# Inverse square roots by Newton steps on VectorE in a four-layer kernel

## The chip, the core and the metric

The kernel runs on one core of a Trainium2 chip. The metric is the device time of one execution in microseconds (us). A core has a matrix engine (TensorE, PE in the profile, with its weight loads shown as PEld), VectorE (DVE), ScalarE (ACT), GpSimd (POOL) and SyncE (SP); each works through its own queue of instructions in order, and semaphores join them.

## What is computed

Four layers are applied to x, 4 x 256 tokens of 256 features, with a context of 4 x 1601 tokens. Each layer adds an attention and then a feed-forward network (FFN) to x, each on a layer-normalized x:

```python
def _layernorm(x, axis=-1, eps=1e-05):
    ...
    return (x - m) / jnp.sqrt(v + eps)
...
        def rms_norm(x, w, eps=EPS):
            var = jnp.mean(jnp.square(x), axis=-1, keepdims=True)
            return x * jax.lax.rsqrt(var + eps) * w
...
    x = x + _L0_xattn_ref(_layernorm(x, axis=-1), ctx_2048, mask_BxS2_bk0)
    x = x + _L0_ffn_ref(_layernorm(x, axis=-1), ...
    x = x + _L1_xattn_ref(_layernorm(x, axis=-1), ctx_2048, ...
    x = x + _L1_ffn_ref(_layernorm(x, axis=-1), ...
    x = x + _L2_xattn_ref(_layernorm(x, axis=-1), ctx_2048, ...
    x = x + _L2_ffn_ref(_layernorm(x, axis=-1), ...
    x = x + _L3_xattn_ref(_layernorm(x, axis=-1), ctx_2048, ...
    x = x + _L3_ffn_ref(_layernorm(x, axis=-1), ...
```

Inverse square roots come in two kinds. A layer normalization needs one for each token. Layers 2 and 3 also normalize each head's query and key by its root mean square: in layer 2 there are 16 query heads and 4 key heads of 128 features, with the keys made from context and tokens; in layer 3 there are 32 heads of 8 features, with keys and values from the context alone. The FFNs are a mixture of 32 experts (layer 0), of 8 with a shared one (layer 1), of 4 (layer 2), and one with quantized weights and activations (layer 3).

## The kernel before, in words

Tokens lie on the 128 partitions; a batch b of 256 tokens is two tiles (q = 0, 1). The four layers run one after the other, and a good deal is pulled forward: layer 2's context keys and values (16 units of batch and key head) are computed as filler for PE (`fill`, tiles fill and filly, `l2_early`, L1206) from layer 0 on and parked in memory. A tile scheduler orders each engine's queue by its own model of costs; only what goes through `pin` or `keep_in_program_order` keeps the written order. A change to a few instructions therefore moves others too.

In the profiled execution the stages lie as follows. Layer 0's attention takes 0 to 130 us and its FFN 130 to about 380. Adding the experts' results (`l0_add`, L544, the gather-adds of L558) and layer 1's attention (`l1_xattn`, L1195: a layer normalization, a summary vector added, a second normalization, then the result added to x at L1204) take about 380 to 516, and layer 1's FFN runs from there to about 625. Layer 2's attention is prepared until 700; its units run from 700 to 1724, about 64 us each. Layer 2's FFN takes 1724 to 1913, layer 3's attention 1913 to 2540, and the rest of its FFN, for the last batch, ends at 2569.

Before the change an inverse square root is `rstd` (L79): a Sqrt on ACT (L81) and a reciprocal on DVE (L82). ACT can evaluate a function only with its table loaded; the profile shows each load as ACT_TABLE_LOAD on the line that called for it. `layernorm` (L84) does bn_stats (L91) and bn_aggr (L92) for both tiles, one rstd, and a normalizing tensor_scalar for each (L95). Other calls are these:

- Layer 0's head (L317): statistics of batch 0, its rstd and transposed tokens; then the statistics of batches 1 to 3 and one rstd for their six tiles. The scores of a batch and tile are masked and their maximum taken by one DVE instruction (L261), the exp on ACT is L271. The decay factor `dec` takes an exp, and its scan on DVE and a DMA from ACT's queue build a row of weights.
- `l2_early`'s `norm` (L1262): one rstd of 13 columns for each early unit.
- Layer 2's `prep` (L1372) prepares a unit while the one before it runs: an rstd over 11 columns (3 key tiles and 8 query columns), then `exps_next` (L1350), a dummy exp that brings the exp table back, then `rq` (L1440), the queries' scaling on POOL (L1442), the keys' scaling on ACT (L1446), transposes (L1452) and copies of kT (L1459). Beside it, for each head, DVE takes the maxima (L1483), ACT the exp p (L1487), POOL scales p (L1522), DVE transposes p (pT, L1528) and PE multiplies by the values.
- Layer 3's `l3_kv` (L1668) makes the keys and values of a batch in 13 steps: two matmuls into a bank, then copies to kr (L1683) and va (L1685); after steps 4, 9 and 12 `l3_squares` (L1716) adds up the squares of 5, 5 and 3 steps (32 heads each, so 160, 160 and 96 columns). For batch 0 one rstd covers all key columns. For later batches the root waits for `queries` (L1779), which takes one Sqrt (L1810) over keys, queries and two columns for the normalization of an older batch, and reciprocals (L1811, L1816). POOL then scales kr.
- In the steady part of layer 3, PE computes the scores of a pair of key tiles, ACT their exp (L1943), PE the product with the values. A generator, `beside` (L1972), puts one piece of other work next to each pair: key and value steps of the next batch, its queries, the FFN of the batch before. These pieces share a single PSUM bank.

Of the kernel before, what the change touches and what calls it, by code (L numbers as in the profile page):

```python
# [11 lines left out]
F32 = mybir.dt.float32  # L12
# [4 lines left out]
I32 = mybir.dt.int32  # L17
AF = mybir.ActivationFunctionType
ALU = mybir.AluOpType
# [4 lines left out]
P = 128  # L24
# [5 lines left out]
NM = 13  # L30
# [10 lines left out]
NH2, NKV2, HD2 = 16, 4, 128  # L41
# [10 lines left out]
FIRST3 = [7, 1, 3]  # L52
# [6 lines left out]
class Kernel:  # L59
# [19 lines left out]
    def rstd(self, out, in_, scale, eps):  # L79

        self.nc.scalar.activation(out, in_, AF.Sqrt, bias=eps, scale=scale)  # L81
        self.nc.vector.reciprocal(out, out)  # L82

    def layernorm(self, out, x):  # L84

        nc = self.nc
        st = self.small.tile([P, 2, 6], F32, name="ln_st")
        mv = self.small.tile([P, 2, 2], F32, name="ln_mv")
        rs = self.small.tile([P, 2], F32, name="ln_rs")
        for q in range(2):  # L90
            nc.vector.bn_stats(st[:, q, :], x[:, q, :])  # L91
            nc.vector.bn_aggr(mv[:, q, :], st[:, q, :])  # L92
        self.rstd(rs, mv[:, :, 1], 1.0, self.eps5)
        for q in range(2):
            nc.vector.tensor_scalar(  # L95
                out[:, q, :], x[:, q, :], mv[:, q, 0:1], rs[:, q : q + 1],
                ALU.subtract, ALU.mult,
            )
# [67 lines left out]
    def l0_xattn(self):  # L166
        nc, tc, i = self.nc, self.tc, self.i
        with ExitStack() as es:
# [142 lines left out]
            for b0, b1 in ((0, 1), (1, B)):  # L311
                for b in range(b0, b1):
                    for q in range(2):
                        st = self.small.tile([P, 6], F32, name="st0")
                        self.pin(nc.vector.bn_stats(st, self.x[b][:, q, :]))
                        self.pin(nc.vector.bn_aggr(mv[:, b, q, :], st))
                self.rstd(rs[:, b0:b1], mv[:, b0:b1, :, 1], 1.0, self.eps5)  # L317
                if b0 == 0:
                    xT = turned(0)
            self.pin(nc.scalar.activation(dec, dec, AF.Exp, scale=-1.0))  # L320
# [885 lines left out]
    def l2_early(self, ctxT):  # L1206
# [88 lines left out]
    def l2_xattn(self):  # L1295
# [11 lines left out]
        with ExitStack() as es:  # L1307
# [42 lines left out]
            def exps_next():  # L1350

                self.pin(nc.scalar.activation(self.small.tile([P, 1], F32, name="one2"), self.eps6, AF.Exp))
# [19 lines left out]
            def prep(u, w, res):  # L1372
# [295 lines left out]
    def l3_kv(self, b, st, early):  # L1668


        nc = self.nc
        ctxT = self.ctx3
        pool = self.late3 if b % 2 else self.a3
        kr = st["kr"] = self.a3.tile([P, NM, D], F32, name="kr3")
        va = st["va"] = self.va3[b % 2]
        ss = st["ss"] = self.a3.tile([P, (NM + 2) * NH3 + 2], F32, name="ss3")
        for m in range(NM):
            copy = nc.scalar.copy if early() else nc.vector.tensor_copy
            tf = self.take()
            for k in range(2):  # L1680
                self.mm(tf, ctxT[:, k, m * P : (m + 1) * P], self.wkv3[:, k, :], k == 0, k == 1)
            tp = tf.rearrange("p (h d c) -> p h d c", d=HD3, c=2)
            copy(kr[:, m, :].rearrange("p (h d) -> p h d", d=HD3), tp[:, :, :, 0])  # L1683
            for h in range(2):
                copy(  # L1685
                    va[h][:, m, : 16 * (HD3 + 1)].rearrange("p (h e) -> p h e", e=HD3 + 1)[:, :, :HD3],
                    tp[:, h * 16 : (h + 1) * 16, :, 1],
                )
# [6 lines left out]
        if b == 0:  # L1695
            nk = NM * NH3
            self.rstd(ss[:, :nk], ss[:, :nk], 1.0 / HD3, self.eps6)
        for m0, m1 in ((0, 4), (4, 8), (8, 12), (12, NM)):
            v = kr[:, m0:m1, :].rearrange("p m (h d) -> p (m h) d", d=HD3)
            f = ss[:, m0 * NH3 : m1 * NH3, None].to_broadcast([P, (m1 - m0) * NH3, HD3])  # L1700
            nc.gpsimd.tensor_tensor(v, v, f, ALU.mult)
        yield
        yield
        yield
        kT = st["kT"] = [pool.tile([P, MP], F32, name="kT3", bufs=2) for _ in range(2)]
        for m0 in range(0, NM, 4):
            for h in range(2):
                n = min(4, NM - m0)
                copy = nc.scalar.copy if early() else nc.vector.tensor_copy
                tp = self.take().rearrange("p (m k) -> p m k", k=P)  # L1710
                for m in range(n):
                    nc.tensor.transpose(tp[:, m, :], kr[:, m0 + m, h * P : (h + 1) * P], self.ident)
                copy(kT[h][:, m0 * P : (m0 + n) * P], tp[:, :n, :].rearrange("p m k -> p (m k)"))
                yield

    def l3_squares(self, st, v, m0, early, pool=None):  # L1716

        n = v.shape[1]
        sq = (pool or self.a3).tile([P, 2 if pool else 5, D], F32, name="sqq3" if pool else "sq3")
        if early:  # L1720
            self.nc.scalar.activation(sq[:, :n, :], v, AF.Square)
        else:
            self.nc.gpsimd.tensor_tensor(sq[:, :n, :], v, v, ALU.mult)
        self.nc.vector.tensor_reduce(
            st["ss"][:, m0 * NH3 : (m0 + n) * NH3], sq[:, :n, :].rearrange("p m (h d) -> p (m h) d", d=HD3),
            AX.X, ALU.add,
        )

    def l3(self, first):

# [10 lines left out]
        with ExitStack() as es:  # L1741
# [16 lines left out]
            def stats(b):  # L1758
                for q in range(2):
                    t = self.small.tile([P, 6], F32, name="st3")  # L1760
                    nc.vector.bn_stats(t, self.x[b][:, q, :])
                    nc.vector.bn_aggr(mv[:, b, q, :], t)
# [9 lines left out]
            def norms(bs):  # L1772

                for b in bs:
                    stats(b)
                v = slice(bs[0], bs[-1] + 1)
                self.rstd(rs[:, v, :], mv[:, v, :, 1], 1.0, self.eps5)

            def queries(b, st, old=None, fill=lambda n: None):  # L1779

                ss = st["ss"]
                nk, nq = NM * NH3, (NM + 2) * NH3
                if old is not None:
                    stats(old)
                    nc.vector.tensor_scalar(
                        ss[:, nq:], mv[:, old, :, 1], float(HD3), HD3 * (1e-5 - 1e-6), ALU.mult, ALU.add
                    )
                elif b:  # L1790
                    nc.vector.memset(ss[:, nq:], 1.0)
                xn = normed(b, rs[:, b, :])
                fill(0)
                tp = bank().rearrange("p (k q t) -> p k q t", k=2, q=2)
# [19 lines left out]
                if b:  # L1814
                    for c in range(0, nk, nk // 2):
                        nc.vector.reciprocal(ss[:, c : c + nk // 2], ss[:, c : c + nk // 2])  # L1816
                fill(2)
                yield
                yield
# [152 lines left out]
            def beside(b, st):  # L1972

                if b + 1 < B:
# [40 lines left out]
            for _ in queries(0, first, None, lambda n: [next(kv) for _ in range(FIRST3[n])]):  # L2015
                pass
            busy = True
            self.take = bank
# [208 lines left out]
```

## Time and profile before

| | us |
|---|---|
| median of 3 runs | 2565.55 (2564.33 to 2566.97) |
| profiled execution | 2571.23 |
| its span | 2569.2 |
| granted TensorE clock in it, mean | 0.973 of full speed |

The profile shows one execution. The busy time of an engine is a sum over all stages, and it is work beside other work for the most part. What a stage is worth is read from what PE waits for in it: a row of the waits names the waiting tile and line, then what it waited for with its line, then the total in us, the number of times and the longest. A group row gives line, engine, operation, tiles and count, then busy us and mean ns of one, then the idle time of the engine just before it and what ended it. A timeline row gives start, duration, engine, line, operation and tiles, with idle time and releaser in brackets.

Busy PE in each stage, and its idle time:

| us | stage | PE busy | PE idle |
|---|---|---|---|
| 0 to 30 | head | 23.88 | 6.12 |
| 30 to 130 | layer 0's attention | 95.38 | 4.62 |
| 130 to 380 | layer 0's FFN | 229.69 | 20.31 |
| 380 to 480 | adding experts, layer 1's attention | 73.28 | 26.72 |
| 480 to 625 | its end, layer 1's FFN | 139.42 | 5.58 |
| 625 to 700 | preparing layer 2 | 66.96 | 8.04 |
| 700 to 1724 | layer 2's units | 1003.27 | 20.73 |
| 1724 to 1920 | layer 2's FFN | 187.03 | 8.97 |
| 1920 to 2130 | layer 3's start and batch 0 | 200.98 | 9.02 |
| 2130 to 2540 | layer 3, batches 1 to 3 | 398.30 | 11.70 |
| 2540 to 2569.2 | end of the last FFN | 11.44 | 17.76 |

### The profile page before, as it was taken

Reading aid. Unit: us, or ns where it says so; the run is one execution under the profiler, and the core shown is the slowest. Engines: PE = TensorE matmul, PEld = TensorE weight load, DVE = VectorE, ACT = ScalarE, POOL = GpSimd, SP = SyncE. Lnnn points to the kernel's source line nnn. Section 1 sums busy time; section 2 is a strip of 40 time slices with the busy share of each in tenths; the row PEclk is TensorE's granted clock in tenths of the full one; section 3 lists DMA queues with packets and bytes.
Section 4 is the critical chain, followed back from the end, with each engine's and each line's share of the span. In section 5 each row is a group of like instructions: output and inputs, shape, how many; then the busy total and the mean of one; then the engine's idle time right before and its main releaser. Section 6 shows DMA issues by size and latency. Waiting matters only on the chain.

```text
span 2569.2 us, 47086 instructions
## 1 busy us (share of the span) xinstructions
PE 2429.6 (95%) x17607; PEld 1507.7 (59%) x17623; DVE 1404.4 (55%) x2915; ACT 1310.9 (51%) x3000; POOL 837.8 (33%) x1516
## 2 busy tenths in 40 slices
PE   8989987899989999999999999998999999999997
PEld 5777865777645555555555555565554544544553
DVE  5453534843567777777777777763324324334323
ACT  3234434533654545454545454423336766757875
POOL 1015644213345555555555555541011001011000
PEclk9999998989999999999999999998999999999998
DMA  7165574624601111111111111004310100000000
GB/s 252 49 211 163 169 151 146 216 91 138 225 18 48 48 48 48 47 47 48 47 48 48 47 48 48 9 1 176 125 56 28 35 1 28 6 1 2 6 6 5
DMA packets 96474, 188.45 MB, mean 73 GB/s; under 512 B 15401, under 2 KB 64297, under 8 KB 95050
## 3 DMA queue, kind: packets, MB, share of 16 engines
q1 hardware_dynamic: 80102, 146.50, 16.7%
q0 software_dynamic: 10416, 28.46, 4.6%
q10 hardware_dynamic: 5732, 10.49, 1.3%
q8 instruction: 143, 2.34, 0.4%
q14 instruction: 81, 0.66, 0.1%
HBM read 137.29 MB, written 48.11 MB: 72 GB/s over the span
## 4 chain that ended last, share of the span: by engine, by line
PE 84%; DVE 5%; ACT 3%; DMA 3%; issue 2%; POOL 1%; another core or an unknown queue 1%; SPq 0%; ACTq 0%; PEld 0%; POOLq 0%; DVEq 0%; PEldq 0%
PE s L77 25%; PE o L77 24%; PE fill L1241 3%; PE f2gu L77 3%; PE b L77 3%; PE f1gu L77 2%; PE acc L77 2%; PE tpq L77 2%; PE f0gu L77 2%; PE filly L1241 2%; PE tpkv L77 2%; PE av L77 2%; PE f0y L77 2%; PE f2y L77 1%; PE f1y L77 1%
## 5 line engine op out<-in xcount | busy, mean ns | idle before, releaser
L1487 ACT ACTIVATE p<-s,nmsm 128x448 f32<-128x448 f32 (+1 forms) x512 | 326.1, 643 | 381.4 <-PE s L77 247.5
L1943 ACT ACTIVATE e<-s 128x1024 f32<-128x1024 f32 (+1 forms) x448 | 404.2, 960 | 159.6 <-PE s L77 154.5
L77 PE MATMUL o<-pT,va 128*128 128x256 f32 (+2 forms) x1920 | 434.2, 379 | 9.4 <-DVE pT L1528 7.9
L77 PE MATMUL s<-kT,qT 128*32 128x448 f32 (+1 forms) x4096 | 427.3, 558 | 11.6 <-ACT kT L1459 8.2
L77 PEld LDWEIGHTS o<-pT,va 128*128 128x128 f32 (+1 forms) x1920 | 347.5, 192 | 130.4 <-issue 89.6
L1522 POOL TENSOR_SCALAR p<-p,rm 128x448 f32<-128x448 f32 (+1 forms) x512 | 323.1, 651 | 6.2
L1483 DVE TENSOR_REDUCE nmsm<-s 128x2 f32<-128x896 f32 (+1 forms) x256 | 287.5, 1123 | 7.9
L77 PE MATMUL s<-qb,kT 32*128 32x256 f32 (+1 forms) x3328 | 268.2, 405 | 13.2 <-ACT e L1943 11.0
L1528 DVE STREAM_TRANSPOSE pT<-p 128x896 f32<-128x896 f32 (+1 forms) x256 | 270.7, 1111 | 9.4 <-POOL p L1522 8.7
L77 PEld LDWEIGHTS s<-kT,qT 128*32 128x32 f32 x4096 | 120.2, 110 | 264.0 <-issue 239.0
L77 PE MATMUL o<-e,va 128*32 128x256 f32 (+1 forms) x3328 | 236.3, 392 | 1.2 <-DVE os L2040 1.2
L77 PEld LDWEIGHTS s<-qb,kT 32*128 32x128 f32 (+1 forms) x3328 | 163.4, 181 | 105.2 <-issue 75.5
L1515 POOL TENSOR_TENSOR rm<-em,tot 32x8 f32<-32x8 f32 x256 | 54.2, 212 | 400.8 <-DVE tot L1512 389.6
L1241 PE MATMUL fill<-wkc_early,ctxT 128*128 128x256 f32 (+1 forms) x572 | 146.2, 407 | 13.4 <-ACT kT_early L1277 12.6
L77 PEld LDWEIGHTS o<-e,va 128*32 128x32 f32 (+1 forms) x3328 | 90.6, 110 | 115.1 <-issue 75.0
L1970 POOL TENSOR_TENSOR x<-x,t 128x32 f32<-128x32 f32 x64 | 14.7, 251 | 439.7 <-DVE t L1965 439.7
L1480 DVE TENSOR_TENSOR s<-s,mask 128x128 f32<-128x128 f32 (+1 forms) x256 | 84.3, 330 | 104.7 <-PE s L77 92.5
L1241 PEld LDWEIGHTS fill<-wkc_early,ctxT 128*128 128x128 f32 (+1 forms) x572 | 114.4, 203 | 35.4 <-ACT kT_early L1277 14.8
L458 POOL DMA_INDIRECT f0xr<-f0xd,f0src x95 | 90.5, 953 | 70.6 <-PE f0tph L515 18.7
L1487 ACT ACTIVATION_READ_ACCUMULATOR p<-s,nmsm 128x1 f32 x512 | 101.4, 198 | 0.0
L77 PE MATMUL f2gu<-f2wgu,f2xsT 128*128 x176 | 85.5, 611 | 0.6 <-ACT f2xsT L74 0.3
L566 POOL DMA_INDIRECT f0yt<-f0yd,f0slot x64 | 62.3, 974 | 64.1 <-DVE x L558 33.4
(488 smaller groups left out, 3500.4 us busy)
## 6 DMA issues: line engine op xcount, KB each, us to landing
ctxT<-in_ctxT SPq DMA_DIRECT2D x9, 1664.0 KB
vd<-va_early SPq DMA_DIRECT2D x96, 128.0 KB
kd<-kT_early SPq DMA_DIRECT2D x48, 256.0 KB
kT<-kd SPq DMA_DIRECT2D x16, 768.0 KB
va<-vd SPq DMA_DIRECT2D x16, 768.0 KB
f0yd<-f0ys SPq DMA_DIRECT2D x95, 128.0 KB
wq<-in_l_wq SPq DMA_DIRECT2D x16, 512.0 KB
wo<-in_l_wo SPq DMA_DIRECT2D x16, 512.0 KB
```

The costliest lines, as they stand in the source:

```text
L77: self.nc.tensor.matmul(out, lhsT, rhs, start=start, stop=stop, **kw)
L458: nc.gpsimd.indirect_dma_start(out=t, out_offset=None, in_=xd[:, :], in_offset=bass.IndirectOffsetOnAxis(ap=src[:, n : n + 1], axis=0),)
L566: nc.gpsimd.indirect_dma_start(out=yt, out_offset=None, in_=yd[:, :], in_offset=bass.IndirectOffsetOnAxis(ap=slot[:, t, r : r + 1], axis=0),)
L1241: ins = nc.tensor.matmul(tp[:rows, t, :], ctxT[u // NKV2][:, k, c0 : c0 + rows], w[u % NKV2][:, k, :], start=k == 0, stop=k == 1,)
L1480: nc.vector.tensor_tensor(sv, sv, mask[:, 2 * c : 2 * c + 2, : nt - CT, :].rearrange("p n t i -> p n (t i)"), ALU.add)
L1483: nc.vector.tensor_reduce(ms[:, 0, 2 * c : 2 * c + 2], s[:, :, : nt * 32], AX.X, ALU.max, negate=True)
L1487: nc.scalar.activation(p[:, n, : nt * 32], s[:, n, : nt * 32], AF.Exp, bias=ms[:, 0, e : e + 1], accum_out=ms[:, 1, e : e + 1],)
L1515: nc.gpsimd.tensor_tensor(r[32 * a : 32 * a + 32], e[:, a], tot, ALU.mult)
L1522: nc.gpsimd.tensor_scalar(p[:, n, : nt * 32], p[:, n, : nt * 32], r[:, e : e + 1], 1.0, ALU.mult, ALU.mult)
L1528: self.pin(nc.vector.transpose(pT[:, 2 * c : 2 * c + 2, :nt, :].rearrange("p n t i -> p n (t i)"), p[:, :, : nt * 32]))
L1943: nc.scalar.activation(e[:kr, :, :n, :], s[t][:kr, :, :n, :], AF.Exp, scale=1.0 / math.sqrt(HD3))
L1970: nc.gpsimd.tensor_tensor(xt, xt, t[:, q], ALU.add)
```

## The change

A new function `root` computes the inverse square root on VectorE alone. It forms v = scale * x + eps, takes a first guess from v's bits (shifted right by one and subtracted from a constant), and makes three Newton steps of three instructions: 12 instructions, each of which needs the result of the one before it.

- `layernorm`, `l2_early`'s `norm`, layer 2's `prep` and layer 3's `norms` call `root` where they called `rstd`. The dummy exp of `prep` goes.
- Layer 0's head keeps the Sqrt for batch 0 and makes one root for each of batches 1 to 3.
- In layer 3 the roots of the keys no longer wait for the queries: each group of 160, 160 or 96 columns has its own root right after its squares, in the scratch space of the squares, and POOL scales that group of kr at once. The queries have a root of their own 64 columns. The normalization of an older batch, whose two columns went with the queries' Sqrt, calls `norms` after the generator has finished keys and queries. The queries' pieces now run together after the first key and value piece that follows the last step.

```diff
+    def root(self, out, in_, scale, eps, space=None):
...
+        vec.tensor_scalar(v, in_, scale, eps, ALU.mult, ALU.add)
+        yi = y.bitcast(I32)
+        vec.tensor_scalar(yi, v.bitcast(I32), 1, None, ALU.arith_shift_right)
+        vec.tensor_scalar(yi, yi, -1.0, float(0x5F3759DF), ALU.mult, ALU.add)
+        for k in range(3):
+            vec.scalar_tensor_tensor(t, y, -0.5, y, ALU.mult, ALU.mult)
+            vec.tensor_tensor(t, t, v, ALU.mult)
+            vec.scalar_tensor_tensor(out if k == 2 else y, t, 1.5, y, ALU.add, ALU.mult)
...
-        self.rstd(rs, mv[:, :, 1], 1.0, self.eps5)
+        self.root(rs, mv[:, :, 1], 1.0, 1e-5)
...
-                self.rstd(rs[:, b0:b1], mv[:, b0:b1, :, 1], 1.0, self.eps5)
+                if b0:
+                    for b in range(b0, b1):
+                        self.root(rs[:, b], mv[:, b, :, 1], 1.0, 1e-5)
+                else:
+                    self.rstd(rs[:, :1], mv[:, :1, :, 1], 1.0, self.eps5)
...
-            self.rstd(ss, ss, 1.0 / HD2, self.eps6)
+            self.root(ss, ss, 1.0 / HD2, 1e-6)
...
-                self.rstd(ss, ss, 1.0 / HD2, self.eps6)
-                exps_next()
+                self.root(ss, ss, 1.0 / HD2, 1e-6)
...
-                self.l3_squares(st, kr[:, m0 : m + 1, :], m0, early())
+                sq = self.l3_squares(st, kr[:, m0 : m + 1, :], m0, early())
+                part = ss[:, m0 * NH3 : (m + 1) * NH3]
+                self.root(part, part, 1.0 / HD3, 1e-6, sq)
+                v = kr[:, m0 : m + 1, :].rearrange("p m (h d) -> p (m h) d", d=HD3)
+                nc.gpsimd.tensor_tensor(
+                    v, v, part[:, :, None].to_broadcast([P, (m + 1 - m0) * NH3, HD3]), ALU.mult
+                )
...
-                v = slice(bs[0], bs[-1] + 1)
-                self.rstd(rs[:, v, :], mv[:, v, :, 1], 1.0, self.eps5)
-
-            def queries(b, st, old=None, fill=lambda n: None):
-
-
+                for b in bs:
+                    self.root(rs[:, b, :], mv[:, b, :, 1], 1.0, 1e-5)
+
+            def queries(b, st, fill=lambda n: None):
...
-                self.l3_squares(st, qr, NM, True, one)
-                part = ss if b else ss[:, nk:nq]
-                nc.scalar.activation(part, part, AF.Sqrt, bias=self.eps6, scale=1.0 / HD3)
-                nc.vector.reciprocal(ss[:, nk : nq + 2 if b else nq], ss[:, nk : nq + 2 if b else nq])
+                sq = self.l3_squares(st, qr, NM, True, one)
+                self.root(ss[:, nk:nq], ss[:, nk:nq], 1.0 / HD3, 1e-6, sq)
...
-                    qs = queries(b + 1, st, b - 1 if b else None)
-                    for _ in range(2):
-                        next(qs)
+                    next(kv)
+                    yield
+                    for _ in queries(b + 1, st):
                         yield
                     for _ in kv:
                         yield
-                    for _ in qs:
-                        yield
-                    nq = (NM + 2) * NH3
-                    old = [normed(b - 1, st["ss"][:, nq:])] if b else []
+                    if b:
+                        norms([b - 1])
+                    old = [normed(b - 1, rs[:, b - 1, :])] if b else []
```

More of the change, by code (lines that the diff above doesn't have):

```diff
@@ L82, in rstd @@
         self.nc.vector.reciprocal(out, out)
+    def root(self, out, in_, scale, eps, space=None):
+        vec = self.nc.vector
+        n = in_.shape[1]
+        if space is not None:
+            space = space.rearrange("p m d -> p (m d)")
+            v, y, t = (space[:, k * n : (k + 1) * n] for k in range(3))
+        else:
+            v, y, t = (self.small.tile([P, n], F32, name=f"root_{a}{n}", bufs=2) for a in "vyt")
+        vec.tensor_scalar(v, in_, scale, eps, ALU.mult, ALU.add)
[6 more added lines that the diff above has]
+            vec.scalar_tensor_tensor(out if k == 2 else y, t, 1.5, y, ALU.add, ALU.mult)
     def layernorm(self, out, x):
@@ L316, in l0_xattn @@
                         self.pin(nc.vector.bn_aggr(mv[:, b, q, :], st))
-                self.rstd(rs[:, b0:b1], mv[:, b0:b1, :, 1], 1.0, self.eps5)
+                if b0:
+                    for b in range(b0, b1):
+                        self.root(rs[:, b], mv[:, b, :, 1], 1.0, 1e-5)
+                else:
+                    self.rstd(rs[:, :1], mv[:, :1, :, 1], 1.0, self.eps5)
                 if b0 == 0:
@@ L1675, in l3_kv @@
         va = st["va"] = self.va3[b % 2]
-        ss = st["ss"] = self.a3.tile([P, (NM + 2) * NH3 + 2], F32, name="ss3")
+        ss = st["ss"] = self.a3.tile([P, (NM + 2) * NH3], F32, name="ss3")
         for m in range(NM):
@@ L1694, in l3_kv @@
             yield
[L1695 to L1701, printed above, removed]
         yield
@@ L1727, in l3_squares @@
         )
+        return sq
     def l3(self, first):
@@ L1775, in norms @@
                     stats(b)
-                v = slice(bs[0], bs[-1] + 1)
-                self.rstd(rs[:, v, :], mv[:, v, :, 1], 1.0, self.eps5)
-            def queries(b, st, old=None, fill=lambda n: None):
+                for b in bs:
+                    self.root(rs[:, b, :], mv[:, b, :, 1], 1.0, 1e-5)
+            def queries(b, st, fill=lambda n: None):
                 ss = st["ss"]
                 nk, nq = NM * NH3, (NM + 2) * NH3
[L1785 to L1791, printed above, removed]
                 xn = normed(b, rs[:, b, :])
@@ L1807, in queries @@
                 nc.vector.tensor_copy(qr, tq)
-                self.l3_squares(st, qr, NM, True, one)
-                part = ss if b else ss[:, nk:nq]
-                nc.scalar.activation(part, part, AF.Sqrt, bias=self.eps6, scale=1.0 / HD3)
-                nc.vector.reciprocal(ss[:, nk : nq + 2 if b else nq], ss[:, nk : nq + 2 if b else nq])
+                sq = self.l3_squares(st, qr, NM, True, one)
+                self.root(ss[:, nk:nq], ss[:, nk:nq], 1.0 / HD3, 1e-6, sq)
                 qrv = qr.rearrange("p q (h d) -> p (q h) d", d=HD3)
                 nc.vector.tensor_tensor(qrv, qrv, ss[:, nk:nq, None].to_broadcast([P, 2 * NH3, HD3]), ALU.mult)
-                if b:
-                    for c in range(0, nk, nk // 2):
-                        nc.vector.reciprocal(ss[:, c : c + nk // 2], ss[:, c : c + nk // 2])
                 fill(2)
@@ L2014, in l3 @@
             norms([0])
-            for _ in queries(0, first, None, lambda n: [next(kv) for _ in range(FIRST3[n])]):
+            for _ in queries(0, first, lambda n: [next(kv) for _ in range(FIRST3[n])]):
                 pass
```

## The prediction

> **What bounds it now.** I read the busy times, the chain that ended last, the table of stages, then in each stage what PE waited for, and last the operations that the change removes. Busy times and chain:
>
> ```profile
> PE 2429.6 (95%) x17607; PEld 1507.7 (59%) x17623; DVE 1404.4 (55%) x2915; ACT 1310.9 (51%) x3000; POOL 837.8 (33%) x1516
> ...
> PE 84%; DVE 5%; ACT 3%; DMA 3%; issue 2%; POOL 1%; another core or an unknown queue 1%; SPq 0%; ACTq 0%; PEld 0%; POOLq 0%; DVEq 0%; PEldq 0%
> ```
>
> PE bounds the kernel, so removed work counts only where PE now waits, and added work only where a PE cover is used up. PE is idle 139.6 us of the span. By stage: head (0 to 30 us) 6.1, layer 0's attention 4.6, 380 to 480 us 26.7 (transfers), layer 2's 1024 us of units only 20.7, start of layer 3 (1920 to 1980) 7.4, its steady part (2130 to 2540) 11.7, tail 17.8.
>
> What goes (ACT groups by line; third column: the idle time before them):
>
> ```profile
> L81 ACT ACT_TABLE_LOAD x34 | 43.6, 1283 | 2.6 <-DVE ln_st L91 1.9
> L1352 ACT ACT_TABLE_LOAD x17 | 21.8, 1283 | 0.3
> L81 ACT ACTIVATE ln_rs<-ln_mv,eps 128x2 f32<-128x2 f32 x24 | 7.1, 297 | 35.3 <-DVE ln_mv L92 29.7 <-DVE ln_st L91 4.8 <-issue 0.8
> ```
>
> With the loads of other lines there are 79; the built order of the changed kernel has 8. 71 x 1.283 = 91 us leave ACT, with some 80 short Sqrts, 16 dummy Exps and four wide Sqrts about 25 us more. ACT is 51% busy, so nearly all of it already lies beside PE. Where it does not, PE's waits name it, here for 2130 to 2540 us:
>
> ```profile
> PE s L77 <- ACT e L1943: 8.4, 3, 3.4
> ```
>
> and for 680 to 1724 us (layer 2's units):
>
> ```profile
> PE s L77 <- ACT kT L1459: 8.2, 15, 0.6
> PE o L77 <- DVE pT L1528: 5.6, 2, 3.4
> PE s L77 <- ACT p L1487: 3.2, 2, 3.0
> ```
>
> **Price of a root.** 83 calls (24 layernorms, 3 at layer 0's head, 16 early norms, 16 units, 12 key groups, 4 queries, 8 norms of layer 3) make 996 VectorE instructions and save about 75 reciprocals. Each needs the one before it. Nearest row: three short dependent instructions in layer 2's router.
>
> ```profile
> 1757.08 0.17 DVE L1019 TENSOR_SCALAR f2wh<-f2cum 128x4 f32<-128x4 f32 x1
> 1757.29 0.17 DVE L1020 TENSOR_SCALAR f2wh<-f2wh 128x4 f32<-128x4 f32 x1
> 1757.37 0.18 DVE L1025 TENSOR_TENSOR f2cum<-f2cum,f2te 128x32 f32<-128x32 f32 x1
> 1757.49 0.17 DVE L1021 TENSOR_SCALAR f2wh<-f2wh 128x4 f32<-128x4 f32 x1
> ```
>
> L1019, L1020, L1021 start 0.21 and 0.20 apart; the independent L1025 fits between at 0.08. So a short root alone takes 12 x 0.21 = 2.5 us; between other work 12 x 0.1 = 1.2. A key group of 128x160: rows of 256 columns (tensor_scalar 0.40, tensor_tensor 0.43, two-step 0.48) and of 64 or fewer (0.17 to 0.22) put one at 0.32 there, 0.36 with its gap: 4.3 us; 128x96 3.3; a query's 128x64 3.0.
>
> [...]
>
> The old path without a load is short. In the tail, aggregate end 2543.46 to reciprocal end 2543.99:
>
> ```profile
> 2543.16 0.30 DVE L1762 BATCH_NORM_AGGREGATE mv<-st 128x2 f32<-128x6 f32 x2
> 2543.82 0.17 DVE L82 RECIPROCAL rs<-rs 128x2 f32<-128x2 f32 x1 [0.36 <-ACT rs L81]
> ```
>
> So where the old path is serial and its table already loaded, a root costs 2.55 - 0.53 = +2.0; where a load is on the path, +0.7; as one item in a busy VectorE queue, 1.2 - 0.16 = +1.0.
>
> **Part by part (plus is slower).**
>
> *Head, +3.5 (+1 to +4).* One Sqrt and reciprocal for tokens 1 to 3 become three roots, 36 instructions. VectorE reads statistics from 12.28 to 15.56, then starts the first mask-and-max (L261) at 17.45 with its scores ready at 15.7; 33 root instructions stand ahead of it. About 8 hide in gaps of 0.1 between statistics, 15 run two-way for 1.6, 7 beside normalizations for 0.5, 6 alone for 1.3, in all 3.4: L261 at about 21. Behind it stand the exp, the freeing of the one score buffer for PE, and the scan whose DMA holds ACT. PE is then nearly unbroken (4.6 idle in 100 us), so the delay stays.
>
> *Layer 0's FFN entry, +1 (0 to +2).* One serial layernorm, +2.0; a fill ahead of PE covers about 3 us, but the router's VectorE chain behind it does not.
>
> *Layer 1's end to its FFN, +8 (+3 to +12).* VectorE is the bound: busy 37.9 of 40 us (479 to 519).
>
> ```profile
> PE tp_ln L127 <- DVE xn L95: 2.0, 1, 2.0
> ```
>
> This is PE's wait for the last of that run. No table loads are here to save (Copy, Square and Sqrt alternate without one). 48 root instructions come between 471.6 and the last gather-add (505.9): 4.9 less 0.6 of reciprocals is 4.3, less about 1.7 of idle time: +2.6. 53 more come between 505.9 and the normalization PE waits for (514.8): 5.8 less 0.5 and a 0.36 hop: +5. POOL's gathers wait for these adds too.
>
> *The FFNs of layers 0 and 1, and 380 to 413 us, 0.* The first two's removed loads stand where PE does not wait; the stretch waits for transfers of the early keys, which no root delays.
>
> *Layer 2's start, -3.5 (-8 to 0).* The first unit's root puts +1.7 and an early norm's +0.4 on paths that PE already waits for. Against that, three loads (685.85, 693.03, 709.22) and the copies queued with them hold ACT's first exps until 710.5, and PE waits 3.0, 2.2 and 3.4 behind them. In the built order exps stand further forward, 5 to 6 us earlier.
>
> *Layer 2's 16 units, 0 (-5 to +6).* One unit's removed ACT work:
>
> ```profile
> 863.48 1.28 ACT L81 ACT_TABLE_LOAD   x1
> 864.78 0.30 ACT L81 ACTIVATE ss<-ss,eps 128x11 f32<-128x11 f32 x1
> 865.10 1.28 ACT L1352 ACT_TABLE_LOAD   x1
> 866.39 0.20 ACT L1352 ACTIVATE one<-eps 128x1 f32<-128x1 f32 x1
> ```
>
> That is 3.1 us of ACT a unit, but PE idles 1.3 us a unit, mostly 0.55 at L1459. The root adds 2 to 3 us to VectorE (76% busy here): transposes of p (L1528) end near 873.5 instead of 872.0, and PE's product needs them at 875.7; the query norm comes at 873.5 instead of 866, and PE's transpose is at 879. Both covered. The upper end: VectorE's 128x8 tensor_scalar L1440 takes 0.51 us here beside POOL, 0.17 elsewhere, so the root could lengthen.
>
> *Layer 2's FFN, 0 (-1 to +1).* Its last layernorm +0.8, under PE's cover; two loads on ACT off the path.
>
> *Layer 3's start, +2 (-3 to +6).* Gone: four loads (1944.18, 1947.16, 1957.66, 1959.67) behind PE waits of 1.9 and 2.7, and a Sqrt that waited in ACT's queue for a transfer ahead of copies, a PE wait of 2.1. New: a serial norm +2.0, a query root +1.8, and about 27 root instructions, one key group among them, between two evacuations of the single bank that PE needs (L1683, L1685): 5 to 7 us of waiting.
>
> *Layer 3 steady, -4 (-8 to +4).* Two queries cost Sqrt and exp loads: at 2147.70 load 1.28, Sqrt 0.70, load 1.28, and PE waits 3.4; a norm makes the third wait: 8.4 all told. [...] Against it 12 key roots in all, half of them in this stretch, stand in front of evacuations on VectorE for 3.3 to 4.3 us, where a step of keys takes about 4: about 0.7 each, 4.4 for the stretch with the query roots. 8.4 - 4.4 = 4.
>
> *Tail, +2 (+1.5 to +2.5).* The serial root; the Sqrt load is prefetched at 2539.92 and the tanh load hidden, so neither gives anything back.
>
> Sum: 3.5 + 1 + 8 - 3.5 + 0 + 0 + 2 - 4 + 2 = +9. The profiled run took 2571.2 (span 2569.2), 5.7 over the median of 2565.55. 2571.2 + 9 = 2580.2; less 5.7: 2574.5.
>
> **Rivals.**
>
> *A: faster, by ACT's freed order.* PE's waits named ACT in layer 2's units (kT 8.2, p 3.2) and layer 3 (8.4, 2.7) all go, with 5 us at layer 2's start, about 27 us gained, while serial roots cost what they must (head, entry, tail, 6) and layer 1's end only half (+4) with layer 3's groups hidden but for 5: -12, 2553. It decides from where ACT's copies kT (L1459) come earlier. For it: 15 waits of one cause. Against it: each is 0.55 and follows PE's own work. Chance 0.17.
>
> [...] Chance 0.23.
>
> *C: VectorE becomes the bound in the steady parts.* Its tensor_scalars beside POOL lengthen by 0.35, three a root, and a unit loses 1 us (16), or each key root costs PE 2 us (24 in all): about +22, 2588. For it: L1440, and xn of L1767 at 1.37 instead of 0.40 beside POOL. Against it: covers of 1 to 3 us a unit. Chance 0.2, within slower.
>
> *Forecast,* +9: chance 0.4.
>
> The range takes B's middle and most of A and C: 2556 to 2591. About 0.2% (5 us) is what a measurement of this kernel can tell from no change. Faster 0.17, same 0.23, slower 0.6.
>
> **What would show it.** 8 table loads and 996 new VectorE instructions at 0.2 alone and 0.1 mixed; L261 first at about 21; the first normalization of layer 1's FFN 7 to 8 us late; PE idle in 700 to 1724 still about 20; the 3.4 waits on e gone, and waits on va or kr copies of 1 to 5 us near 1945 to 1970 and with each key group; the tail 2 longer. Wrong if PE idle in the units falls by 8 (A), if L1440-like slowing shows on the roots (C), or if dependent short instructions follow each other at 0.1.

## The result, and the profile after

The changed kernel is slower: 2600.79 us (2600.59 to 2607.52, 4 runs) beside 2565.39 us (2564.33 to 2566.97), a ratio of 1.0141 (1.0125 to 1.0157), +35.4 us. Forecast were +9 and a range of 2556 to 2591: the direction was right, the size was not, and the time lies outside the range.

Busy times and the chain that ended last, of the profiled execution after (2600.59 us, span 2598.9):

```profile
PE 2432.5 (94%) x17623; PEld 1506.3 (58%) x17623; DVE 1555.7 (60%) x3836; ACT 1202.1 (46%) x2847; POOL 838.3 (32%) x1512
...
PE 81%; DVE 11%; issue 3%; DMA 2%; ACT 2%; POOL 1%; another core or an unknown queue 1%; SPq 0%; ACTq 0%; DVEq 0%; POOLq 0%
```

PE did the same work. ScalarE lost 109 us (1310.9 to 1202.1) and VectorE took on 151 (1404.4 to 1555.7), and VectorE's share of the chain went from 5 to 11%.

Where the time went is read by taking the same PE instruction in both traces and subtracting its starts. The delay that PE has gathered, in us:

| at (us of before) | delay | change in the stage | forecast |
|---|---|---|---|
| 60, past the head | +2.3 | +2.3 | +3.5 |
| 180, layer 0's FFN entered | +4.4 | +2.1 | +1 |
| 360, layer 0's FFN done | +2.2 | -2.2 | 0 |
| 540, layer 1's FFN entered | +13.3 | +11.1 | +8 |
| 760, layer 2's units running | +11.0 | -2.3 (by way of about +21 at 690) | -3.5 |
| 1700, the units done | +11.0 | 0.0 | 0 |
| 1900, layer 2's FFN done | +6.2 | -4.8 | 0 |
| 1990, layer 3 started | +16.4 | +10.3 | +2 |
| 2520, layer 3's steady part done | +27.6 | +11.1 | -4 |
| 2560, tail | +29.6 | +2.0 | +2 |

The last column sums to +9, the third to +29.6, which is the difference of the spans (2598.9 - 2569.2) to 0.1. The medians differ by 35.4, because the profiled run of before was 5.7 us over its median and that of after was not. The -4.8 in layer 2's FFN belongs to this: 3.7 of it is PE's busy time, and the granted clock was 0.90 in before's trace from 1715 to 1835 us and 0.93 in after's over the same instructions (1726 to 1842). An experiment below (l3_only) runs the very program of before up to 1900 us, and its PE was 5.1 us earlier there, 3.1 of them lost in before's trace in this FFN.

Layer 1's end and layer 3 carry the loss. The waits of PE after, first 413 to 535 us, then 1930 to 2010, then 2100 to 2540 (waiting tile and line, what it waited for, total, times, longest; the smaller rows are left out):

```profile
PE tp_ln L146 <- DVE xn L114: 14.3, 1, 14.3
```

```profile
PE b L77 <- DVE va L1707: 4.7, 1, 4.7
PE b L1832 <- DVE qr L1824: 2.5, 2, 1.6
PE b L1810 <- DVE xn L1789: 2.3, 1, 2.3
PE b L77 <- DVE qT L1833: 1.5, 1, 1.5
```

```profile
PE b L77 <- DVE va L1707: 16.2, 6, 3.6
PE b L1832 <- DVE qr L1824: 3.2, 2, 1.6
```

The first was 2.0 before. At layer 3's start (1913 to 2000 us) PE waited before for these:

```profile
PE s L77 <- ACT e L1943: 2.7, 1, 2.7
PE fill L77 <- ACT va L1685: 2.1, 1, 2.1
PE b L77 <- DVE va L1685: 1.9, 1, 1.9
```

In the steady part the 8.4 us of waiting for e are gone as forecast, and 16.2 us of waiting for copies of va and 3.2 for qr stand in their place. One of the six waits for va, on VectorE (start, duration, line):

```profile
2150.72 1.49 DVE L1745 TENSOR_REDUCE ss<-sq 128x160 f32<-128x1280 f32 x1 [2.04 <-POOL sq L1744]
2152.24 0.24 DVE L94 TENSOR_SCALAR sq<-ss 128x160 f32<-128x160 f32 x1
...
2155.84 0.42 DVE L1705 COPY kr<-b 128x256 f32<-128x256 f32 x1
2156.17 0.32 DVE L101 SCALAR_TENSOR_TENSOR ss<-sq 128x160 f32<-128x160 f32 x1
2156.40 0.48 DVE L1707 COPY va<-b 128x128 f32<-128x128 f32 x2
```

and on PE:

```profile
2149.83 1.98 PE L77 MATMUL b<-wkv,ctxT 128*128 128x512 f32 x4
...
2157.03 3.34 PE L77 MATMUL b<-wkv,ctxT 128*128 128x512 f32 x4 [3.63 <-DVE va L1707]
```

PE has filled the one bank at 2151.8 and has nothing else to do from 2153.4 on. The sum of squares and the root hold VectorE until 2155.8, and only then are kr and va copied out of the bank and PE may fill it again. Four of the six waits are like this one (two of 3.6 us and two of 2.3, 11.8 in all), behind the key roots of 160 columns. The key roots of 96 columns come after the last step, and no wait stands behind them. The other two waits, 2.2 each, are of another kind. Here the older batch's normalization, which no longer goes with the queries' Sqrt, comes ahead of a key copy with its root and the quantization of its tokens for the FFN:

```profile
2106.13 0.17 DVE L94 TENSOR_SCALAR root_v<-mv 128x2 f32<-128x2 f32 x1
...
2111.23 0.35 DVE L1877 TENSOR_SCALAR xn<-xn,xq3r 128x256 f32<-128x256 f32 x1
2111.49 0.42 DVE L1705 COPY kr<-b 128x256 f32<-128x256 f32 x1
```

```profile
2112.45 2.29 PE L77 MATMUL b<-wkv,ctxT 128*128 128x512 f32 x3 [2.19 <-DVE va L1707]
```

The PE rows also show a second cost. The four matmuls of a key step take 1.98 us at 2149.83 (granted clock 1.00) and 3.34 behind the wait of 3.63 (0.56); at layer 3's start they take 3.78 behind the wait of 4.7 (0.50). Over the instructions that run from 1925 to 1950 us in before, the granted clock was 0.93 before and 0.81 after, and PE was busy 3.8 us longer. This is over a third of what layer 3's start loses. l3_only, l3_late and stretch_old below, which have the new start, show the same 3.7 to 4.0, and l3_old, which has the old one, shows none. That the waits bring the lower clock on was not tested apart.

### The profile page after: what moved, and what is told of

The parts are those of the page before. It is cut to its first block, busy times and chain, and to the rows that moved or that the text cites. A ratio compares the mean times of both kernels' runs of the same rounds, so it can differ in the third digit from the quotient of the medians.

```text
span 2598.9 us, 47869 instructions
## 1 busy us (share of the span) xinstructions
PE 2432.5 (94%) x17623; PEld 1506.3 (58%) x17623; DVE 1555.7 (60%) x3836; ACT 1202.1 (46%) x2847; POOL 838.3 (32%) x1512
## 4 chain that ended last, share of the span: by engine, by line
PE 81%; DVE 11%; issue 3%; DMA 2%; ACT 2%; POOL 1%; another core or an unknown queue 1%; SPq 0%; ACTq 0%; DVEq 0%; POOLq 0%
PE s L77 24%; PE o L77 23%; PE f2gu L77 3%; PE b L77 3%; PE fill L1264 3%; PE f0gu L77 2%; PE acc L77 2%; PE tpq L77 2%; PE f1gu L77 2%; PE tpkv L77 2%; PE av L77 2%; PE f0y L77 2%; PE f2y L77 1%; PE filly L1264 1%; PE f1y L77 1%
## 5 line engine op out<-in xcount | busy, mean ns | idle before, releaser
L1978 POOL TENSOR_TENSOR x<-x,t 128x32 f32<-128x32 f32 x64 | 14.7, 250 | 448.0 <-DVE t L1973 448.0
L1264 PE MATMUL fill<-wkc_early,ctxT 128*128 128x256 f32 (+1 forms) x572 | 147.0, 409 | 12.2 <-ACT kT_early L1300 7.0
L1283 DVE TENSOR_REDUCE ss_early<-sq_early 128x4 f32<-128x512 f32 x64 | 37.2, 582 | 86.1 <-ACT sq_early L1282 70.7
```

What stands on the lines that cost most here:

```text
L1264: ins = nc.tensor.matmul(tp[:rows, t, :], ctxT[u // NKV2][:, k, c0 : c0 + rows], w[u % NKV2][:, k, :], start=k == 0, stop=k == 1,)
L1978: nc.gpsimd.tensor_tensor(xt, xt, t[:, q], ALU.add)
```

## The experiments

Theory after the result: a root takes the time that the prediction charged for it, but in two stretches something waits right behind it in VectorE's queue, so most of this time counts. These are the stretch from the first gather-add to layer 1's FFN, and layer 3's key steps. Rivals: VectorE is slowed everywhere by GpSimd; the new order of layer 3's pieces does it; the transfers near 400 us do it.

The groups of runs were made on different chips: the kernel before took 2566.74 us in the first group, 2523.07 in the second, 2524.49 in the third and 2570.3 in the fourth, each beside the kernels of that group. Ratios are to these.

**Layer 3 as before, everything else changed (l3_old).** Edit: `l3_kv`, `queries`, `norms` and `beside` of the kernel before in the changed one.

> The changed kernel with layer 3 as before (Sqrt and reciprocal for keys, queries and norms, the old order of its pieces); all other roots stay. Theory (roots stand in VectorE's queue ahead of the copies that free the one bank): layer 3 is worth 23 us of the 35 (start 10, steady 11, tail 2), so about 2578. Rival (the loss is spread, VectorE slower everywhere beside GpSimd): less than 12 us come back, 2589 or more.

Measured 2583.61, ratio 1.0068 (1.0051 to 1.0086). By the ratio 1.0141 the whole change would take 2602.9 on that chip, so about 19 of 36 us come back: less than the 23 expected, and more than the 12 that a loss spread everywhere would leave. Its trace runs parallel to before's through all of layer 3, at +13.4 us from 1920 to the end. **Only layer 3 changed (l3_only):**

> The kernel before with only layer 3 changed (key groups, queries, norms, their new order). Theory: +23 us, about 2588, with six waits of PE on copies of va of 2 to 4 us. Rival (layer 3 loses only because ACT and VectorE arrive late and in another order from layers 0 to 2): under +12, below 2577.

Measured 2587.6, 1.0083 (1.0063 to 1.0103), +20.9. Its waits from 2050 us on begin with the row of the changed kernel to the digit (va, 16.2 in six, the longest 3.6). By its trace the start of layer 3 loses 10.3, each of the two later key batches 6.6, the tail 2.0, and the older norm's missing table loads give back 2.4. So layer 3's loss is its own and doesn't depend on the layers ahead of it. Up to 1900 us this is the kernel before.

**Where the key roots stand.** Both edits are made on l3_only and keep the written order of copies and roots on VectorE. l3_split cuts each root in three and makes a third behind the copies of each following step:

```diff
+            next(todo, None)
             if m in (4, 9, NM - 1):
...
-                self.root(part, part, 1.0 / HD3, 1e-6, sq)
+                todo = parts(part, sq, m0, m + 1)
```

> The kernel before with layer 3 changed, but each key root cut into three pieces of four to six instructions, each piece held behind the copies of the next key and value step by the kept program order on VectorE. Same instructions, another place. Theory (place in the queue): the waits on va go (16 us in the steady part, 4.7 at the start), the gain of the absent table loads stays: about 2568. Rival (it is the amount of VectorE work, or the new order of the pieces of other work): no better than 2583 beside 2587.6 for the same change uncut.

l3_late makes the roots whole, in the three pieces after the last step:

```diff
-                self.root(part, part, 1.0 / HD3, 1e-6, sq)
+                parts.append((part, m0, m + 1))
...
+        for part, m0, m1 in parts:
+            self.root_pinned(part, part, 1.0 / HD3, 1e-6, sq)
...
+            yield
```

> The same, with the three key roots whole, but only after the last key and value step, one in each of the three pieces that follow. Theory: no copy of kr or va waits any more, one or two copies of the queries or of a head's result wait up to 4 us: about 2571. Rival (amount of work or order of pieces): 2583 or more.

Measured: l3_split 2533.71, 1.0041 (1.0028 to 1.0054), +10.6; l3_late 2527.94, 1.0018 (1.001 to 1.0025), +4.9; beside +20.9 for the same instructions where the change put them. So for the key roots the place decides, and the amount of VectorE work does not. Of the expected sizes (+1 and +4 over before) that of l3_late was met; l3_split stayed 10 us slower than expected; its trace loses 6 us more than l3_late's at layer 3's start. PE's waits of l3_late from 2050 to 2510 us, without the rows of the last FFN:

```profile
PE b L77 <- DVE va L1724: 5.1, 4, 2.2
PE b L1849 <- DVE qr L1841: 3.2, 2, 1.6
```

The 16.2 became 5.1. The 11.8 behind key roots shrank to two waits of 0.36, as before had them. The other 4.4 are the two waits behind the older batch's normalization and quantization, which this edit leaves where the change put them. So the rival of layer 3's new order may hold for a part: 4.4 of the 16.2 us come from this chain at its new place, with 2.3 us of root in it each time. Place and root were not separated; with half the root, in newton1, such a wait is still 1.7. The queries' root costs its two waits of 1.6. What is left of l3_late's loss is at layer 3's start: against before's trace it loses 8.8 us there, with a wait for va of 4.8, gains 4.0 in the steady part and loses 1.9 in the tail.

**Half the length (newton1).** Edit, in `root`; two of three Newton steps are left out:

```diff
-        for k in range(3):
+        for k in range(1):
```

> The changed kernel with one Newton step in each root instead of three, so 6 instructions instead of 12; the other two steps are left out, and the roots are less exact. Theory (the loss is the time of a root where something waits behind it): layer 1's end falls from 11 to about 5, each key group's wait by 2.1, so layer 3 from 23 to about 0; 2570 in all. Rival (the loss comes with the order of work and not with the length of a root): 2590 or more.

Measured 2514.82, 0.9969 (0.996 to 0.9977): 8 us faster than before. The two stretches did what was expected: by the traces layer 1's end loses 4.3 us instead of 12.6 (newton1 and, of the third group, after_again against l3_late, 360 to 500 us), and layer 3 takes 1.1 longer than in unit_only, where it is as before. The total was 13 us better than expected: layer 2's start gained 7 us where the changed kernel gains 2.3, and its trace is ahead by 7 us at 180 us already, the cause of which was not separated.

**The rest of the changed kernel.** ln_old has Sqrt and reciprocal back in `layernorm`, head_old in layer 0's head:

> The changed kernel with Sqrt and reciprocal back in the layer normalizations only. Theory: layer 1's end gives back its 11 us and layer 0's FFN entry 1, with their table loads hidden as before: about 2589. Rival (the early key norms' roots, which stay, fill the same queue): 5 us or less come back, 2595 or more.

> The changed kernel with one Sqrt and reciprocal for batches 1 to 3 at the head. Theory: the delay of 2.4 us that PE carries from the head on comes back, 2598. Rival (a later wait for transfers near 380 us swallows it): unchanged, 2600 to 2601.

ln_old: 2590.94, 1.0098 (1.0079 to 1.0117), about 12 us of the 36. The sum came as expected and the place did not. PE's wait for xn is 5.0 instead of 14.3, but other waits take most of that back (va of the early keys 9.9 us for 5.0, and 2.4 for kr, which is new), and the gain comes from layer 0's FFN entry (4.6) and layer 2's preparation (6.6). head_old: 2600.61, 1.0141 (1.012 to 1.0162). The 2.7 us at the head do come back in its trace, and at 540 us PE is 1.1 us behind where it was in the changed kernel. Here an earlier head doesn't make layer 1's end earlier.

**Layer 1's end.** One kind of root alone on the kernel before, the change once more on the same chip, and the change without the roots of this stretch:

```diff
-        self.root(rs, mv[:, :, 1], 1.0, 1e-5)
+        if self.tight:
+            self.rstd(rs, mv[:, :, 1], 1.0, self.eps5)
+        else:
+            self.root(rs, mv[:, :, 1], 1.0, 1e-5)
```

and the same in the early `norm` (stretch_old; `tight` holds from the first gather-add to layer 1's FFN).

> The changed kernel once more, unaltered, beside the two partial versions and the kernel before on one chip. If the losses lie in fixed places of the program (theory): 30 to 36 us over the kernel before, with layer 3 costing 21 to 23 of it again. If the loss depends on how the transfers near 400 us happen to lie (rival): layer 1's end costs much less than 11 us where these transfers are quicker.

> The kernel before with the root in the 24 layer normalizations only. Theory as predicted (roots of the layer normalizations load VectorE at layer 1's end): +5 to +11 there and +1 to +2 at layer 0's FFN entry, +6 in layer 2's preparation: 10 us or more slower in all. Rival (at layer 1's end it is the early keys' roots that count): no more than 3 us at that place.

> The kernel before with the root in the 16 early key norms of layer 2 only. Theory as predicted: at layer 1's end two or three of them add 2 to 3 us, elsewhere they hide: 0 to 3 us slower. Rival (they are what holds VectorE and the transposes behind it at layer 1's end): 8 us or more slower, lost between 400 and 520 us.

> The changed kernel with Sqrt and reciprocal in those layer normalizations and early norms only that are issued between the first gather-add of layer 0's experts and the entry of layer 1's FFN. Theory (VectorE's queue is full in this whole stretch, so each root adds its time): the 11 to 13 us lost there come back, about 15 us from the first gather-add to PE's transposes; a part of it is lost again at layer 2's start, so 5 to 11 us faster than the changed kernel, 22 to 28 over the kernel before. Rival (order of the fills or the transfers): the stretch stays over 8 us longer than before.

| kernel | ratio | first gather-add to PE's tp_ln, us | root instructions in it | VectorE idle in it, us |
|---|---|---|---|---|
| before, first trace | | 101.6 | 0 | 19.8 |
| after, first trace | 1.0141 | 116.3 | 197 | 14.9 |
| stretch_old | 1.0062 (1.0042 to 1.0082) | 101.5 | 0 | 19.6 |
| l3_late (as before here) | | 88.1 | 0 | 6.2 |
| early_only | 0.9987 (0.9977 to 0.9996) | 95.5 | 78 | 4.6 |
| ln_only | 1.0039 (1.0024 to 1.0053) | 100.3 | 113 | 5.5 |
| after_again | 1.0127 (1.011 to 1.0144) | 104.0 | 197 | 3.1 |
| newton1 | 0.9969 | 93.7 | 96 | 3.6 |

In the first two rows the transfers ahead of this stretch are slow (120 GB/s from 375 to 413 us of before, 123 from 377 to 415 us of after), and stretch_old's stretch is as long as before's; the rows from l3_late on are of the second and third groups (222 GB/s at that place in l3_late). In l3_late VectorE is busy 82 of 88 us before any root is added, and the roots lengthen the stretch: 78, 113 and 197 instructions by 7.4, 12.2 and 15.9 us. That they don't add up fits the price of a root, though no run tests this alone. A lone early root (13 columns) in after_again takes 2.5 us, with the next dependent instruction 0.21 later; where two roots go side by side, two instructions start in 0.20:

```profile
389.41 0.17 DVE L97 TENSOR_SCALAR root_y<-root_y 128x13 int32<-128x13 int32 x1
389.62 0.17 DVE L99 SCALAR_TENSOR_TENSOR root_t<-root_y 128x13 f32<-128x13 f32 x1
```

```profile
483.55 0.28 DVE L101 SCALAR_TENSOR_TENSOR root_y<-root_t,root_y 128x2 f32<-128x2 f32 x2
483.75 0.28 DVE L99 SCALAR_TENSOR_TENSOR root_t<-root_y 128x2 f32<-128x2 f32 x2
```

In stretch_old, without its 197 roots, the stretch is as long as before to 0.1 us and PE's wait for xn is 2.0 again:

```profile
PE tp_ln L150 <- DVE xn L118: 2.0, 1, 2.0
```

So these root instructions are the whole of what the stretch grew; transfers and the order of the fills aren't needed. stretch_old took 2585.45, +15 over before, where 22 to 28 were expected. By its trace it stays 16 to 19 us ahead of the changed kernel to the end, since nothing is lost again at layer 2's start. The rival of quicker transfers failed too: where they are quicker, VectorE is idle for 6.2 us instead of 19.8, and the roots lengthen the stretch by 15.9 us instead of 14.7. In total after_again took 2556.77 (1.011 to 1.0144), +32, of it 21 in layer 3.

Of the two alone, ln_only took 2535.56, +11, as expected in sum: about 14 lost at this end, and 6 given back at layer 2's start. early_only took 2521.59, 3 us faster than before, which neither expectation had: it loses 7 here and gains 8 at layer 2's start, where Sqrts of its kind were; its trace is also 3.5 us ahead at 180 us, unexplained.

**Layer 2's units alone (unit_only, unit_again).** Edit on the kernel before:

```diff
-                self.rstd(ss, ss, 1.0 / HD2, self.eps6)
-                exps_next()
+                self.root(ss, ss, 1.0 / HD2, 1e-6)
                 rq = two.tile([P, 8], F32, name="rq2")
```

> The kernel before with the root only in the 16 units of layer 2, the dummy exps gone; 32 table loads (41 us of ScalarE) less. Theory (they lay beside PE's work): between 2562 and 2567, PE's idle time in the units within 3 us of before. Rival (ScalarE's copies of kT come earlier): 8 us or more faster, 2558 or less. Other rival (VectorE becomes the bound beside GpSimd): 2575 or more.

> The kernel before with the root only in the 16 units, once more. The first look gave a ratio of 0.995. If the gain is the 10 to 11 us at layer 2's start that its trace shows: 8 to 11 us faster than before again. If it was the luck of four runs: within 4 us of before.

Measured 2511.51, 0.9952 (0.9935 to 0.9968), and on another chip 2558.14, 0.9949 (0.9934 to 0.9964): 12 us faster than before both times. My theory of "same" was wrong and the number of the rival right, but not its reason. Between 760 and 1700 us PE waits as ever for kT, in unit_again and in before:

```profile
PE s L77 <- ACT kT L1477: 9.0, 14, 1.0
```

```profile
PE s L77 <- ACT kT L1459: 7.7, 14, 0.6
```

The units themselves gain nothing: PE loses 1.7 us in them in unit_again, by its delay against before at 760 and 1700 us. The gain lies at layer 2's start (10 us by the second group's traces, 620 to 720 us; 6 by unit_again's trace against the first of before, 620 to 760 us, and 10 by best2's). There the table loads (1.28 us each) stood ahead of the first exps: in before's trace one runs from 709.22 us and the first p starts at 710.51. Counted from the last f1y matmul of layer 1's FFN, the first exp p comes at 85.4 us in l3_late, which is as before here, and at 81.6 in unit_only; the 32nd at 135.3 and 125.4. Of PE's waits there (690 to 760 us), 5.6 for pT and 3.2 for p before, unit_again has these:

```profile
PE o L77 <- DVE pT L1546: 2.5, 3, 1.5
PE s L77 <- ACT p L1505: 0.2, 1, 0.2
```

The edit takes away the loads, the Sqrts and the dummy exps together, so their parts in the gain are not told apart.

**A mixed version (best, best2).** The units' roots, and in layer 3 the late key roots and queries of batches 1 to 3 and the normalizations of older batches; the rest by Sqrt. best2 makes layer 3's first norm by a root as well:

```diff
-            norms([0])
+            norms([0], True)
```

> The kernel before with the root where ScalarE's loads were in somebody's way and VectorE has room: the 16 units of layer 2 without the dummy exps, and in layer 3 the queries of batches 1 to 3, their keys after the last key and value step, and the older batches' normalizations; everything at the head, the layer normalizations, the early norms, batch 0 of layer 3 and the tail stay with Sqrt. Theory (place decides): 10 to 12 us from layer 2's start and 4 to 6 from layer 3, so 14 to 18 us faster than before. Rival (gains at layer 2's start are used up by later waits): 8 us or less faster.

> The mixed version (best) with one thing changed: the first normalization of layer 3 by a root. Theory (in best its Sqrt waited at the head of ScalarE's queue for x, with copies of va behind it, PE waited 7.4 us): that wait shrinks to 2 to 3 us, so about 5 us faster than best, 7 to 10 us faster than before. Rival (the new order of keys and queries costs it): no gain over best.

best: 2521.67, 0.9992 (0.9983 to 1.0): 3 us faster where 14 to 18 were expected, so the theory failed here. In it a Sqrt at layer 3's start waits for x at the head of ScalarE's queue, with copies behind it, and PE waits:

```profile
1872.80 0.29 ACT L81 ACTIVATE rs<-mv,eps 128x2 f32<-128x2 f32 x1 [10.29 <-DVE mv L1811]
```

```profile
PE fill L77 <- ACT va L1723: 7.4, 1, 7.4
```

best2: 2557.4, 0.995 (0.9935 to 0.9965). The row is gone, and waits of 2.4 for va and 2.3 for xn are there. It beats before by 13 us, more than the 7 to 10 expected, but not unit_again (2558.14 beside it): by its trace against before's, layer 3 loses 4.2 us up to 2130 us and gains 5.9 from there to 2520.

## Why the prediction was wrong

*Right.* The length of the roots: a lone root of two columns took 2.3 us (2.5 forecast), a key group 4.25 (4.3), 128x96 3.3 (3.3), a query's 3.0 (3.0). The table loads were 8 after, of 1.283 us each. The first mask-and-max of the head came at 20.2 us (21). The units: PE's delay is +11.00 at 760 and at 1700 us. The head (+2.3 for +3.5), the tail (+2.0) and the end of the waits for e (8.4) came as argued, and so did layer 2's start in kind: exps further forward against roots on serial paths.

*Layer 3 steady, forecast -4, measured +11.1.* The step that failed is "about 0.7 each" for a key root against the evacuation. The root's 4.3 us were set against a step's 4 us, as if nearly a whole step were cover. In the wait shown above the cover is 1.6 us (2151.8 to 2153.4), of which the copies need 1.0; the sum of squares (1.49) stands in the queue as well. The four roots of 160 columns in this part cost 11.8 us of waiting, 2.9 each; the two of 96 cost none. Two terms were missing or too small: the older batch's normalization and quantization ahead of a key copy (4.4, put at nothing) and the two query roots (3.2, put at 0.2 together). 11.8 + 4.4 + 3.2 - 8.4 is 11.0. l3_split and l3_late show that for the key roots it is the place.

*Layer 3's start, forecast +2, measured +10.3.* The right waits were listed and priced singly (norm 2.0, query 1.8, 5 to 7 for the bank), and the 6.7 of old waits taken off. Measured were 4.7 for va, 2.3 for xn and 2.5 for qr, with 1.5 and 1.2 for the query copies that follow, and 1.4 of the wait for e stayed. By the waits this is 13.6 for 7.5 before (6.7 and 0.8 for qT), +6.1. The other 4 us had no term in the prediction: PE's busy time, longer by 3.8 at a granted clock of 0.81 instead of 0.93. l3_late shows that the start loses even with the key roots moved. Which part of it is the new order of keys and queries was not separated.

*Layer 1's end, forecast +8, measured +11.1, and 16 to 19 us of the whole by stretch_old.* The failing step is "VectorE is the bound: busy 37.9 of 40 us (479 to 519)": the full queue was read from one window, and 101 root instructions after 471 us were counted. What counts is the queue from the first gather-add (413.6) on, with 197. From there the stretch grew by 14.7 us: 8.9 ahead of the last gather-add, where +2.6 was put, and 5.8 behind it, for +5.

*Size of the sum.* The stages of the two traces differ by 29.6 us and the medians by 35.4. The prediction took the 5.7 us that before's profiled run had over its median to be in the profile of after as well. They were not: after's profiled run lies at its median. 3.7 us of before's excess are PE's busy time at the lower clock in layer 2's FFN; the rest was not traced.

*Range.* It was drawn round 2566, the time of a balance of gains and losses, with a chance of 0.23. No run of the changed kernel shows the balance: the stages add up to +29.6 us, layer 1's end alone to +11.1, and a lone root took 2.3 us.

Rival C was the nearest in number (2588) and named the key roots at 2 us each; the six of the steady part cost 2.0 on the mean. Its chance was 0.2. Its other half, slower units, didn't happen, although the sign named for it did: root instructions became longer in the units (last section). A's gain at layer 2's start exists (unit_again). In the changed kernel little of it is left (2.3), and with the layer normalizations by Sqrt (ln_old) 6.6 more come out between 620 and 760 us.

## What to carry to other kernels

In this kernel, moving a short function from one engine to another was priced by what stood behind it in the new queue, not by the load of that engine: the same 12 instructions cost nothing in layer 2's units, and 2.3 to 3.6 us of PE's waiting in front of the only copy that frees its bank, with a lower granted clock behind the longer waits (0.56 behind 3.63 us, 0.50 behind 4.7). Look for how far back a full queue reaches before counting what is added to it. Take the part that pays (here the units, 0.5% faster) and leave the engine's old work where it was hidden.

## What the runs showed that was not expected

Tiny VectorE instructions became long beside GpSimd here. In the changed kernel at layer 3's start:

```profile
1964.76 2.37 DVE L100 TENSOR_TENSOR root_t<-root_t,root_v 128x2 f32<-128x2 f32 x1
```

```profile
1964.58 2.52 POOL L1717 TENSOR_TENSOR kr<-kr,ss 128x1280 f32<-128x1280 f32 x1 [7.07 <-DVE root_t L99]
```

Two columns took 2.37 us instead of 0.16, to 1967.13, and GpSimd's scaling of kr ends at 1967.10. In the units the shift L96 (128x11) took 0.84 on the mean of 16 (0.94 at 875.33, beside GpSimd's L1454, 1.00 at 875.23) where 0.16 to 0.19 is its length elsewhere (2 and 13 columns). In the units of the changed kernel the longer root instructions cost PE nothing (its delay is +11.00 at both ends).

The stretch from 360 to 480 us is 38 us shorter on the chips of the second and third groups (l3_late against before, the same program there), which is most of what separates 2523 from 2566 us.
